# When eight small filler writes enter the transfer queue of a mixture-of-experts kernel

## The chip, the cores and the metric

The kernel runs on one core of a Trainium2 chip. The metric is the device time of one execution in microseconds (us); the number that counts is the median over several executions. Engines are named as in the profile: PE is TensorE (PEld its weight loads), DVE is VectorE, ACT is ScalarE, POOL is GpSimd, SP is SyncE, which in this kernel only issues transfers (DMAs). All data is float32.

## What is computed

One transformer layer: layer norm and cross attention (32 heads, 8 key and value groups) with a residual, then layer norm and a feed-forward block made of one shared expert and eight routed experts of which each token uses two. Cut to the part around the change:

```
x = x + xattn(layernorm(x), ctx, ctx, Wq, Wk, Wv, Wfc, bfc)      # 8 x 256 tokens, 512 wide
h = layernorm(x).reshape(2048, 512)
scores = softmax(h @ gate_weight.T)                              # 8 experts
w, i   = two best experts out of the two best of four groups
routed = sum over the two: w * (silu(h @ gate_w[i].T) * (h @ up_w[i].T)) @ down_w[i].T   # inner width 352
shared = (silu(h @ sh_gate_w.T) * (h @ sh_up_w.T)) @ sh_down_w.T                         # inner width 704
x = x + routed + shared
```

## The kernel before

**Two phases.** `attention` does the attention, the shared expert and the router for one batch after another. The router gives each token, for each of its two experts, a row in a table `rows` in device memory: expert `e` owns a stretch that begins at row `e * S_R`, and POOL scatters the normed token, its weights and its number there (`send`, L1173). When the last token has its place, `plan` (L1184 to L1267) works out on DVE where each expert's rows end (`t_end`) and which expert and first row each later tile of 128 rows has (`t_exp`, `t_row`).

`routed` then runs over tiles of 128 rows. The first eight tiles are the first 128 rows of expert 0, 1, ... 7, with addresses known when the program is built; tiles from number 8 on take expert and row out of the plan. A tile `i` goes through these helpers:

- `load(i)` (L407, L413) issues five transfers from `rows`: four of 64 KB into `xs`, and one of 8 KB into `mark`.
- `turn(i)` (L434 to L451) transposes `xs` on DVE into `rxT` and copies the weight and the token number.
- `up(i)` (L468, L483, L485) multiplies by gate and up weights on PE (`rg`), takes the silu on ACT (`rsg`) and the product on DVE (`ract`).
- `turn_act(i)` (L491 to L494) transposes `ract` on PE into `ra` and copies it on DVE to `raT`.
- `down(i)` (L499, L510, L513) multiplies by the down weights (`ro`), scales (`ry`) and lets POOL add the rows to the output.

`run` writes the order out by hand. At step `n` it issues the load of tile `n + 2`, turns tile `n + 1`, and runs up of tile `n`, down of tile `n - 1`, and the transpose of `ract(n)`. On DVE, in which order is fixed, `turn(n + 1)` therefore stands ahead of `ract(n)`; on PE `ra(n)` waits for `ract(n)`.

**Weights.** All routed weights stay in SBUF: `up_weights(e)` is one transfer of 1408 KB (L381) and `down_weights(e)` one of 768 KB (L384). Those of experts 0 to 2 are asked for at the end of the attention phase, with the loads of tiles 0 to 2; step `n` asks for those of expert `n + 3`. At step 5 `second` (L428, L429) fetches another 1408 and 768 KB for a tile that is shared by two experts.

**Empty rows.** An expert's last tile can reach past its rows. `blank` is a table of 64 rows of zeros in device memory with harmless token numbers, and for each expert one transfer copies it behind the expert's last row (L575, 132 KB, memory to memory). `value` reads the address on SP out of `t_end` (L372). `alone` says that the scatters and these eight writes need not wait for one another, since no two of them write the same row. It says nothing on loads, which read the same table `rows`.

**SP's queue.** All of these transfers are issued by SP in the order of the program. Before the change SP's order from the end of attention on is:

```
up(0) down(0) load(0) load(1) up(1) down(1) load(2) up(2) down(2)
8 x [ read t_end, blank -> rows ]
act of the last batch -> kept                       (L199, 768 KB)
step 0: up(3) down(3)
step 1: load(3) up(4) down(4)
step 2: load(4) up(5) down(5) ...
```

Here up(e) and down(e) stand for the weight transfers. Each of SP's transfers signals one of eight semaphores in turn.

Of the kernel before, what the change touches and what calls it, by code (L numbers as in the profile page):

```python
# [60 lines left out]
N_EXP, F = 8, 352  # L61
# [24 lines left out]
def xattn_ffn(  # L86
# [46 lines left out]
    )  # L133
    left.close()
    routed(
        ctx, tc, ps_m, wgu, wd, wsd, kept, ident,
        rows, t_exp, t_row, t_one, t_all, t_end, blank, out, tail, right,
# [211 lines left out]
def alone(tc, dma):  # L349
    tc.declare_no_dep(dma, group="rows", reason="no two of them write the same row")  # L350
    tc.add_to_no_dep_group("rows", dma)


def routed(
# [16 lines left out]
    def value(table, i, engine, top, p=0):  # L371
        return nc.values_load(  # L372
            table[p : p + 1, i : i + 1],
            engines=(engine,),
            min_val=0,
            max_val=top,
            skip_runtime_bounds_check_because=because,
        )

    def up_weights(e):  # L380
        nc.sync.dma_start(wgu_all[:, e], wgu[e])  # L381

    def down_weights(e):
        nc.sync.dma_start(wd_all[:, e], wd[e])  # L384
# [11 lines left out]
    def load(i):  # L396


        xs[i] = place(early, [P, P // BAND, P], "xs", f"xs{i}", 3)
        marks[i] = place(early, [P, W - D], "mark", f"mark{i}", 3)  # L400
        k = i - N_EXP
        step = R if k >= N_FULL else P
        for p in range(0, P, step):
            first = i * S_R if k < 0 else value(t_row, k, ENG.SP, N_EXP * S_R, p)
            some = slice(p // BAND, (p + step) // BAND)
            for r in range(NC):
                nc.sync.dma_start(  # L407
                    xs[i][r * BAND : (r + 1) * BAND, some],
                    rows[bass.ds(first, step), r * P : (r + 1) * P].rearrange(
                        "(m i) d -> i m d", i=BAND  # L410
                    ),
                )
            nc.sync.dma_start(marks[i][p : p + step], rows[bass.ds(first, step), D:])  # L413

    def two(a, m, b, n):

        t = others.tile([P, len(SCH) * (D + S)], F32, tag="two", name="two")
        return (
            t[:, : a * m].rearrange("p (a m) -> p a m", m=m),
            t[:, a * m : a * m + b * n].rearrange("p (b n) -> p b n", n=n),  # L420
        )
# [3 lines left out]
    def second(i):  # L425
        e = value(t_exp, i - N_EXP, ENG.SP, N_EXP - 1, R)
        seconds[i] = wgu_2, wd_2 = two(NC, 2 * F, len(FCH), D)
        nc.sync.dma_start(wgu_2, wgu[bass.ds(e, 1)].rearrange("o p c f -> p (o c) f"))  # L428
        nc.sync.dma_start(wd_2, wd[bass.ds(e, 1)].rearrange("o p c d -> p (o c) d"))  # L429

    def turn(i):

        xTs[i] = place(early, [P, NC, P // BAND, BAND], "xT", f"rxT{i}")
        nc.vector.transpose(  # L434
            xTs[i].rearrange("p c m i -> p m c i"),
            xs.pop(i).rearrange("p m (c j) -> p m c j", j=BAND),
        )
        row = marks.pop(i)

        w1s[i] = place(early, [P, 1], "w1", f"rw1_{i}", 5)  # L440
        if i < N_EXP:
            nc.vector.tensor_copy(w1s[i], row[:, i : i + 1])
        else:
            wt = place(early, [P, N_EXP], "wt", f"rw{i}")
            nc.vector.tensor_mul(wt, row[:, :N_EXP], t_one[:, i - N_EXP])
            nc.vector.tensor_reduce(w1s[i], wt, AX.X, ALU.add)
        ids[i] = []
        for part, _ in halves(i, None):
            to = place(early, [P, 1], f"id{part.start}", f"rid{i}_{part.start}", 6, I32)
            to = to[: part.stop - part.start]  # L450
            nc.vector.tensor_copy(to, row[part, W_ID - D : W_ID - D + 1].bitcast(I32))  # L451
            ids[i].append(to)
# [23 lines left out]
    def up(i):  # L476
        of_expert(i)
        gu = [ps_g.tile([P, F], F32, tag=f"g{k}", name=f"rg{i}_{k}") for k in range(2)]
        for k in range(2):
            product(gu[k], i, slice(k * F, (k + 1) * F))  # L480
        del xTs[i]
        sg = place(work, [P, F], "sg", f"rsg{i}")
        nc.scalar.activation(sg, gu[0], AF.Silu)  # L483
        acts[i] = place(work, [P, F], "act", f"ract{i}")
        nc.vector.tensor_mul(acts[i], gu[1], sg)  # L485
# [35 lines left out]
    def down(i):  # L521
        o = ps_y.tile([P, D], F32, tag="y", name=f"ro{i}")
        for fc, (_, fn) in enumerate(FCH):
            down_chunk(o, i, fc, fn)
        add_up(o, i)

    def last(i, before):


        of_expert(i)  # L530
        g = ps_g.tile([P, F], F32, tag="g0", name=f"rg{i}_0")
        product(g, i, slice(0, F))
        sg = place(work, [P, F], "sg", f"rsg{i}")
        nc.scalar.activation(sg, g, AF.Silu)
        down(before)
        a = place(work, [P, F], "act", f"ract{i}")
        aTs[i] = place(work, [P, len(FCH), P], "aT", f"raT{i}")
        o = ps_y.tile([P, D], F32, tag="y", name=f"ro{i}")

        def values_of(fc):  # L540
            f0, fn = FCH[fc]
            u = ps_g.tile([P, F], F32, tag=f"g{int(fc < 2)}", name=f"ru{i}_{fc}")[:, :fn]
            product(u, i, slice(F + f0, F + f0 + fn))
            nc.vector.tensor_mul(a[:, f0 : f0 + fn], u, sg[:, f0 : f0 + fn])

        def turned(fc):
            f0, fn = FCH[fc]
            ps = ps_m.tile([P, P], F32, tag="m", name=f"ra{i}_{fc}")
            nc.tensor.transpose(ps[:fn], a[:, f0 : f0 + fn], ident)
            nc.vector.tensor_copy(aTs[i][:fn, fc], ps[:fn])  # L550

        values_of(0)
        values_of(1)
        turned(0)
        values_of(2)
        turned(1)
        down_chunk(o, i, 0, FCH[0][1])
        turned(2)
        for fc in (1, 2):
            down_chunk(o, i, fc, FCH[fc][1])  # L560
        del xTs[i]
        add_up(o, i)
# [7 lines left out]
        up_weights(e)  # L570
        down_weights(e)

    for e in range(N_EXP):
        to = value(t_end, e, ENG.SP, N_EXP * S_R)
        alone(tc, nc.sync.dma_start(rows[bass.ds(to, R), :], blank).ins)  # L575
    while tail.cost < tail.total - 2 * 0.88:
        tail.step()
    turn(0)
# [30 lines left out]
    def run(tiles):  # L609

        halfs = [n for n, i in enumerate(tiles) if i >= N_EXP + N_FULL]
        when = [N_EXP - 3, *(n + 3 for n in halfs)]
        for n, i in enumerate(tiles):
            if 3 <= n + 2 < len(tiles):
                load(tiles[n + 2])
            if i + 3 < N_EXP:
                up_weights(i + 3)
                down_weights(i + 3)
            for k, at in zip(halfs, when):
                if at == n:  # L620
                    second(tiles[k])
            if n + 1 == len(tiles):
                last(i, tiles[n - 1])
                break
            if n == halfs[-1] + 2:
                down_sh, act_sh = two(len(SCH), D, len(SCH), S)
                nc.sync.dma_start(down_sh, wsd)
                nc.sync.dma_start(act_sh, kept)
            if n > 0:
                turn(tiles[n + 1])  # L630
            up(i)
            if n > 0:
                down(tiles[n - 1])
            else:
                turn(tiles[n + 1])
            turn_act(i)

        sums = []
        for q in range(QC):
            t0 = ((B - 1) * QC + q) * P  # L640
            to = out[t0 : t0 + P, :]
            sums.append((to, work.tile([P, D], F32, tag=f"sum{q}", bufs=1, name=f"sum{q}")))
            nc.sync.dma_start(sums[q][1], to)
        for q, (to, y) in enumerate(sums):
            ps = ps_m.tile([P, D], F32, tag="m", name=f"o{B - 1}_{q}")
            for i in range(len(SCH)):
                nc.tensor.matmul(  # L647
                    ps,
                    lhsT=act_sh[:, i, q * P : (q + 1) * P],
                    rhs=down_sh[:, i],  # L650
                    start=(i == 0),
                    stop=(i == len(SCH) - 1),
                )
            nc.vector.tensor_add(y, ps, y)
            nc.sync.dma_start(to, y)
        more()
# [4 lines left out]
    for k in range(RUN_HALF):  # L661
        tiles.insert(N_EXP + 4 + 7 * k, half[k])
    run(tiles)


# [825 lines left out]
```

## Time and profile before

| | us |
|---|---|
| median of 3 runs | 940.75 (939.1 to 941.12) |
| profiled execution, its own time | 938.76 |
| span of the profiled execution, first to last instruction | 937.0 |
| PE busy | 910.8 (97%) |
| DVE busy | 475.0 (51%) |
| ACT busy | 182.3 (19%) |
| POOL busy | 134.3 (14%) |
| mean granted TensorE clock | 0.993 |

The span is 1.8 us shorter than the profiled execution's own time, and that execution is 2.0 us below the median of the three runs. Times below are counted from the first instruction of the span. The routed phase begins on PE at 635.07 us, so it fills about the last third. The PE row of a profile counts time in which PE works; a time in which PE stands still while a transfer is under way shows as a dip in that row and as a step "DMA" in the chain of work that ended last.

### The profile page before, as it was taken

How to read it: one execution, taken by the hardware profiler on the slowest of the kernel's cores; microseconds unless marked ns; L12 is line 12 of the kernel's file. 1: busy time of each engine (PE TensorE's matmuls, PEld its weight loads, DVE VectorE, ACT ScalarE, POOL GpSimd, SP SyncE). 2: the span in 40 equal slices, each digit the busy share in tenths (PEclk: the TensorE clock that was granted, in tenths of full speed). 3: DMA queues.
4: the chain of work that ended last, by engine and by line, in shares of the span. 5: the costliest groups of instructions: out<-in, count | busy, mean ns of one | idle time of the engine just before them, and what ended most of it. 6: DMA issues, size and time to landing. Idle time of an engine off the chain costs nothing.

```text
span 937.0 us, 13140 instructions
## 1 busy us (share of the span) xinstructions
PE 910.8 (97%) x4865; PEld 531.1 (57%) x4865; DVE 475.0 (51%) x1063; ACT 182.3 (19%) x222; POOL 134.3 (14%) x171
## 2 busy tenths in 40 slices
PE   9999999999999999999999999999599999999997
PEld 8775565536445554654654544775355555555553
DVE  4554867566755856654675655382233333333331
ACT  1224123223223222222222241101000000000000
POOL 4000100201101101010120121030012212121211
PEclk9999999999999999999999999999799999999999
DMA  6366620201102021011111011069995364644623
GB/s 223 86 180 220 192 46 2 82 6 35 48 13 81 24 46 47 1 53 35 36 48 35 13 48 57 12 219 294 347 341 105 69 164 71 157 78 87 149 38 75
DMA packets 59266, 90.45 MB, mean 97 GB/s; under 512 B 13312, under 2 KB 39680, under 8 KB 57152
## 3 DMA queue, kind: packets, MB, share of 16 engines
q1 hardware_dynamic: 50512, 70.63, 24.7%
q0 software_dynamic: 7648, 17.83, 9.4%
q10 hardware_dynamic: 1040, 1.12, 0.4%
q8 instruction: 41, 0.67, 0.3%
q14 instruction: 25, 0.20, 0.1%
HBM read 57.88 MB, written 27.24 MB: 91 GB/s over the span
## 4 chain that ended last, share of the span: by engine, by line
PE 89%; DVE 4%; DMA 3%; SPq 1%; issue 1%; ACT 1%; POOL 0%; ACTq 0%; DVEq 0%; POOLq 0%
PE rg L468 16%; PE gu L181 14%; PE ro L499 9%; PE o L205 8%; PE s L988 7%; PE s L955 7%; PE fc L1046 6%; PE pq L921 6%; PE av L1007 6%; PE pkv L865 2%; DVE nm L964 1%; PE pkv L854 1%; PE ra L491 1%; PE o L647 1%; PE tn L972 1%; PE warm L1279 1%
## 5 line engine op out<-in xcount | busy, mean ns | idle before, releaser
L964 DVE TENSOR_REDUCE nm<-s 128x8 f32<-128x2048 f32 x64 | 146.6, 2290 | 86.2 <-PE s L955 82.0
L468 PE MATMUL rg<-wgu_all,rxT 128*128 (+2 forms) x552 | 171.3, 464 | 1.1 <-DVE rxT L434 0.9
L181 PE MATMUL gu<-hT,gu_w 128*128 128x256 f32 x704 | 166.6, 385 | 0.0
L996 ACT ACTIVATE ex<-s 128x2048 f32<-128x2048 f32 x64 | 120.1, 1877 | 225.7 <-PE s L988 216.0
L181 PEld LDWEIGHTS gu<-hT,gu_w 128*128 128x128 f32 x704 | 129.1, 190 | 40.9 <-issue 24.6
L468 PEld LDWEIGHTS rg<-wgu_all,rxT 128*128 128x128 f32 (+1 forms) x552 | 100.6, 187 | 56.4 <-issue 8.8
L499 PE MATMUL ro<-wd_all,raT 128*128 (+5 forms) x210 | 96.5, 594 | 0.0
L513 POOL DMA_INDIRECT y<-ry,rid x38 | 58.4, 1537 | 239.5 <-DVE ry L510 156.0
L205 PE MATMUL o<-down,act 128*128 128x512 f32 x168 | 79.6, 604 | 0.3 <-DVE q L346 0.3
L988 PE MATMUL s<-qT,kT 17*128 17x512 f32 x512 | 73.0, 640 | 2.0 <-DVE nm L964 1.9
L955 PE MATMUL s<-kT,qT 16*128 16x256 f32 x1024 | 73.4, 400 | 1.5 <-ACT ex L996 0.8
L483 ACT ACTIVATE rsg<-rg 128x352 f32<-128x352 f32 x34 | 15.8, 464 | 253.2 <-PE rg L468 246.0
L955 PEld LDWEIGHTS s<-kT,qT 16*128 16x128 f32 x1024 | 46.3, 184 | 30.9 <-ACT ex L996 14.1
L499 PEld LDWEIGHTS ro<-wd_all,raT 128*128 128x128 f32 (+3 forms) x210 | 38.4, 186 | 42.9 <-issue 35.5
L921 PE MATMUL pq<-xT,wq_sb 128*128 128x256 f32 x256 | 61.2, 386 | 0.5 <-DVE acc L214 0.3
L1007 PE MATMUL av<-ex,v 128*32 128x512 f32 x512 | 61.5, 598 | 0.0
L1046 PE MATMUL fc<-wfc_sb,o 128*128 128x512 f32 x128 | 60.9, 604 | 0.1
L1173 POOL DMA_INDIRECT rows<-lnf,idx x32 | 31.7, 991 | 201.0 <-DVE idx L1167 190.2
L485 DVE TENSOR_TENSOR ract<-rg,rsg 128x352 f32<-128x352 f32 x34 | 17.8, 523 | 84.0 <-PE rg L468 84.0
L510 DVE TENSOR_SCALAR ry<-ro,rw 128x512 f32<-128x512 f32 x35 | 26.3, 750 | 66.7 <-PE ro L499 66.7
L921 PEld LDWEIGHTS pq<-xT,wq_sb 128*128 128x128 f32 x256 | 46.6, 190 | 14.5 <-issue 6.0
L205 PEld LDWEIGHTS o<-down,act 128*128 128x128 f32 x168 | 29.4, 190 | 35.8 <-issue 34.5
(184 smaller groups left out, 710.0 us busy)
## 6 DMA issues: line engine op xcount, KB each, us to landing
wgu_all<-wgu SPq DMA_DIRECT2D x8, 1408.0 KB
xs<-rows SPq DMA_DIRECT2D x128, 64.0 KB
wd_all<-wd SPq DMA_DIRECT2D x8, 768.0 KB
two<-wgu SPq DMA_DIRECT2D x3, 1408.0 KB
cT<-ctxT SPq DMA_DIRECT2D x8, 512.0 KB
acc<-x SPq DMA_DIRECT2D x16, 256.0 KB
y<-acc SPq DMA_DIRECT2D x16, 256.0 KB
x<-x SPq DMA_DIRECT2D x14, 256.0 KB
```

Of the source, the lines that this page charges most:

```text
L181: nc.tensor.matmul(ps[:, i], lhsT=self.gu[k][:, c, i * P : (i + 1) * P], rhs=hT[:, c], start=(c == 0), stop=(c == NC - 1),)
L205: nc.tensor.matmul(ps, lhsT=act[:, k, q * P : (q + 1) * P], rhs=self.down[:, k], start=(i == 0), stop=(i == len(SCH) - 1),)
L468: nc.tensor.matmul(dst[part], lhsT=xTs[i][:, c, part.start // BAND : part.stop // BAND], rhs=w, start=(c == 0), stop=(c == NC - 1),)
L499: nc.tensor.matmul(o[part], lhsT=aTs[i][:fn, fc, part], rhs=w, start=(fc == 0), stop=(fc == len(FCH) - 1),)
L513: nc.gpsimd.indirect_dma_start(out=out, out_offset=bass.IndirectOffsetOnAxis(ap=to, axis=0), in_=y[part], in_offset=None, compute_op=ALU.add,)
L921: nc.tensor.matmul(ps[:, i], lhsT=wq_sb[:, c, part], rhs=xT[:, c], start=(c == 0), stop=(c == NC - 1),)
L955: nc.tensor.matmul(ps[:, r, j], lhsT=qT[band, G, j0 + j, qc * P : (qc + 1) * P], rhs=kT[band, G], start=True, stop=True,)
L964: nc.vector.tensor_reduce(nms[b, G, j0][:, qc], ps, AX.X, ALU.max, negate=True)
L988: nc.tensor.matmul(ps[:, r], lhsT=kT[band, G, kc * P : (kc + 1) * P], rhs=qT[band, G, j0 : j0 + 2], start=True, stop=True,)
L996: nc.scalar.activation(ex, ps, AF.Exp, scale=HD**-0.5)
L1007: nc.tensor.matmul(av[32 * r : 32 * r + 32], lhsT=vs[b % DEEP][:, kc, 4 * G + r], rhs=ex[:, r], start=(kc == 0), stop=(kc == QC - 1),)
L1046: nc.tensor.matmul(ps, lhsT=o[:, c, qc * P : (qc + 1) * P], rhs=wfc_sb[:, c], start=(c == 0), stop=(c == NC - 1),)
```

## The change

The eight writes of empty rows become a helper `empties(e)`, and they move. They were issued all together between the weights of expert 2 and `kept`. Now step `n` of `run` issues two of them behind its weights, for experts `2n` and `2n + 1`: two each at steps 0, 1, 2 and 3, and none later. The number, the size and the addresses of the writes are the same.

```diff
@@ routed
-    for e in range(N_EXP):
+    def empties(e):
+
         to = value(t_end, e, ENG.SP, N_EXP * S_R)
         alone(tc, nc.sync.dma_start(rows[bass.ds(to, R), :], blank).ins)
+
     while tail.cost < tail.total - 2 * 0.88:
         tail.step()
     turn(0)
@@ run
             if i + 3 < N_EXP:
                 up_weights(i + 3)
                 down_weights(i + 3)
+            for e in range(N_EXP)[2 * n : 2 * n + 2]:
+                empties(e)
             for k, at in zip(halfs, when):
                 if at == n:
                     second(tiles[k])
```

SP's order after it:

```
... load(2) up(2) down(2)
act of the last batch -> kept
step 0: up(3) down(3) blank 0, 1
step 1: load(3) up(4) down(4) blank 2, 3
step 2: load(4) up(5) down(5) blank 4, 5
step 3: load(5) up(6) down(6) blank 6, 7
step 4: load(6) up(7) down(7)
```

## The prediction

> **What bounds the kernel now.** First the page's slices, for where PE stands still:
>
> ```profile
> PE   9999999999999999999999999999599999999997
> PEclk9999999999999999999999999999799999999999
> DMA  6366620201102021011111011069995364644623
> ```
>
> A slice is 23.4 us. PE is full but for slice 29 (656 to 679 us), the start of the routed phase, where the granted clock falls too. DMA is at nine tenths in slices 28 to 30. Then the chain of waits around this dip:
>
> ```profile
> 651.97 3.81 DMA rows<-blank
> 655.80 0.33 SPq L407
> ...
> 657.52 8.64 DMA xs<-rows
> ...
> 667.19 0.44 DVE ract L485
> 667.63 0.04 issue
> 667.68 0.90 PE ra L491 x3
> 668.58 6.48 PE rg L468 x16
> 675.06 2.58 PE ro L499 x6
> 677.64 0.33 PE ra L491 x3
> ```
>
> PE's idle 11.1 us ends with `ra(2)`, which waits for `ract(2)`, which stands on DVE behind `turn(3)`, which waits for `xs` of tile 3. That load was issued at 655.80, when the last empty-row write had landed. So the writes are in the chain today. SP's part of the timeline:
>
> ```profile
> 640.59 0.33 SPq L384 DMA_DIRECT2D wd_all<-wd  x1
> 644.42 8.06 SPq L575 DMA_DIRECT2D rows<-blank  x8
> 652.57 0.53 SPq L199 DMA_DIRECT2D kept<-act  x1
> 653.15 0.45 SPq L381 DMA_DIRECT2D wgu_all<-wgu  x1
> 653.64 0.64 SPq L384 DMA_DIRECT2D wd_all<-wd  x1
> 655.80 2.15 SPq L407 DMA_DIRECT2D xs<-rows  x4
> ```
>
> The eight writes hold SP for 8.06 us, 1.0 us each. Two waits show. The first write begins only when the last piece of load(2) has landed (its semaphore is full at 644.29): a write waits for every earlier load of `rows`. And load(3) waits for the semaphore of the eighth write, although it reads the first 128 rows of expert 3: a load waits for earlier writes of `rows`. Lastly the windows of the transfers:
>
> ```profile
> 648.00:650.00 2.00, 2.00 (x9) 1.00 0.87 318
> 650.00:652.00 2.00, 2.00 (x8) 1.00 0.42 134
> 652.00:654.00 2.00, 2.00 (x8) 1.00 0.88 136
> 654.00:656.00 2.00, 2.00 (x6) 1.00 1.10 367
> ```
>
> The last two columns are DMA share and GB/s: a hole of some 4 us, because SP issues the small writes more slowly than they move, and then a full stream.
>
> From 656 to 706 us the routed phase lives on that stream. By the landings in the trace (last of 16 marks), mark of tiles 3, 4, 5, 6, 7 lands at 666.3, 673.7, 682.2, 690.2, 698.3: 8.0 us per tile, against 7.65 on PE (0.33 + 4.74 + 2.58 in the chain). The slack is used up by tile 8: `turn(8)` starts at 706.42, `ract(7)` ends at 707.87, PE is ready for `ra(7)` at 708.04. So each us by which the stream is later at tile 8 is a us of the end; a us earlier counts only if it is earlier there too.
>
> **The change, part by part.** *Removed:* 8.06 us of SP, and the hole. In order: down(2) stays at 640.59. `kept` follows, when down(1)'s semaphore is full at 643.08; up(3) and down(3) by 644.5; then two reads of `t_end` and two writes by 646.7. The stream doesn't stop now: down(2) lands at 650.8 as before, `kept` 2.4 later (before: 655.78 to 658.16), up(3) 3.8 later (658.16 to 661.95), down(3) 2.7 (to 664.68), two writes at 0.35 (successive writes at 651.45 and 651.77). Sum: 660.3.
>
> *Added: load(3) waits for writes 0 and 1, which lie behind up(3) and down(3) in the queue.* It goes out at 660.3, not at 655.8, but into an empty queue: its last `xs` is issued 1.7 us on and lands 1.85 later (706.92 to 708.75, an empty stretch), so 663.9 in place of 666.16. `ra(2)` comes at 665.4 instead of 667.7. So far a gain of 2.3 us.
>
> *Added: the same wait three more times, and its mirror.* Writes 2 and 3 wait for load(3) to land (T + 3.7, counting from the load's issue T). On SP up and down(4) are ahead of them, so nothing useful is held up; but their data queue behind those weights, and load(4) stands behind them on SP and waits until they have landed. All that comes after load(4), up(5) included, waits with it, and the queue runs dry. The period from load to load:
>
> - five issues of load: 2.3 us (664.75 to 667.02)
> - up from issue to landing in a nearly empty queue: 6.3 us (up(1): 634.25 to 640.57)
> - down: 2.5 us (up(1) at 640.57, down(1) at 643.08)
> - two writes: 0.7 us, and 0.1 until SP goes on
>
> Together 11.9, with POOL's scatters in the queues about 12.0, against 8.0 today. The writes' own issues (T + 3.8 to T + 5.8) lie beside the weights and cost nothing. Without cover they would cost 2 us a pair.
>
> So T is 660.3, 672.3, 684.3, 696.3 for loads 3 to 6. Their `xs` land 3.6 later: 663.9, 675.9, 687.9, 699.9. `ra(i)` follows 1.3 us after the landing of `xs(i + 1)` (666.38 to 667.68) if PE is ready: `ra(3)` at 677.2 (before 677.5), `ra(4)` 689.2 (685.1), `ra(5)` 701.2 (692.8). Load(7) waits for no write and follows up and down(7) in the stream (T + 11.2 + 1.5 = 709.0 against 698.3); the two transfers of `second` and load(8) follow at the 8.0 of today, 717.0 against 706.3. `ra(7)` comes at 718.3 against 708.04.
>
> **Sum: +10.3 us at tile 8, rounded to +10.** After it PE is the bound with full buffers as before (load(9) lands 5 us ahead of its use), so nothing is won back.
>
> *A rule on order.* In the trace writes issued from 644.42 on land behind down(2): the first write's marks begin at 648.56, down(2)'s at 648.26, 4 us after the write's issue. [...] If writes overtook the weights, they would land 3.2 us after issue (the seventh write, 650.94 to 654.16), at T + 8.0: the next load would be out before the weights are through, and the period would be today's. [...] I take the row, since the writes kept their place behind the weights there.
>
> *A rule on the clock.* The 11.1 us of idle PE were followed by half clock from 661.7 to 672.0, and `rg(3)` took 6.68 us instead of 4.90. [...] While the stream is the bound a tile at half clock (7.65 + 1.8 to 2.7) still fits into 12.0; only behind the last stop would 0 to 4 us come on top. [...]
>
> **The rivals.** *Faster: the transfers flow on.* One mechanism: no new load waits behind weights, because the writes land early or are not tied to them. Then `xs(3)` follows in the stream at 661.9, 4.3 earlier than today, and three more pairs of writes give back 3 x 0.7: -2.2 at tile 8, thus 938.6 us. For it: the hole of 4 us goes away with certainty. Against it: load(3) waits for the eighth write's semaphore today. It decides if a write lands within about 8 us of the load before it, or if load(4) is issued before down(4) has landed.
>
> *Only part of the stops.* The first pair gains as I say, but the period is nearer 9.5 to 10.5, since up takes 3.1 to 3.8 us once data flow and the latency is smaller behind the landing loads. Four periods then lose less: +3 to +6, about 945. Against it are up(0) and up(1), 6.1 and 6.3 us in nearly empty queues.
>
> *More.* Half clock behind the last stop, and slower writes: +13 to +17, about 955.5.
>
> **How the numbers follow.** The main case has 0.72 (its own range 947.5 to 953.5), part of the stops 0.12, faster 0.10, more 0.06. The profiled execution took 938.76 (span 937.0), so its twin would take 948.8; against the median of 940.75, 2.0 above that execution, the forecast is 940.75 + 10 = 950.7. The range 944 to 955 takes in the main case, most of the partial one and the edge of the last. What can be told from no change is about 0.2%, 1.9 us: faster by more has 0.09, within it 0.03 (the edges of the faster and the partial case), slower 0.88.
>
> **What would show it.** Right: `kept` issued near 643 us, up(3) right behind it; load(3)'s wait at L407 put down to the writes at about 660; loads 3 to 6 some 12 us apart; low DMA shares of 2 to 3 us around each; `ra(2)` about 2 us earlier; two or three PE idles of about 4 us, ended by `ract` behind `turn`, where there was one of 11. Wrong: loads 4 to 6 issued 8 us apart and one short PE idle (the faster rival), or PE idle at tiles beyond 8, which nothing in my sum makes.

## The result

The changed kernel takes 951.34 us (median of 4 runs, 949.07 to 952.2) against 940.93 (median of 4): 10.4 us slower, ratio 1.0107, 95% interval 1.008 to 1.0134. The forecast was 950.7. The profiled execution took 952.2, its span is 950.5. First the page's slices, now 23.8 us wide:

```profile
PE   9999999999999999999999999986779999999996
PEclk9999999999999999999999999999889999999998
DMA  6377610200101111102011001278786364644623
```

One slice of half-idle PE (slice 29 before) has become three of six or seven tenths (slices 28 to 30, 642 to 713 us), and the transfers, at nine tenths there before, are down to seven or eight. The chain of waits in that stretch says what PE waits for now:

```profile
646.67 12.29 DMA rows<-blank
658.98 0.35 SPq L407
...
660.80 1.88 DMA mark<-rows
...
663.92 7.77 DMA rows<-blank
...
671.77 0.34 SPq L407
...
676.67 6.66 DMA rows<-blank
...
688.26 8.77 DMA rows<-blank
...
697.10 0.33 SPq L407
```

Four times the chain goes through the landing of a write of empty rows; before it did so once. SP's timeline shows the order of issue (start, duration, line, names, count), with L576 for the writes (L575 before):

```profile
642.77 0.33 SPq L199 DMA_DIRECT2D kept<-act  x1
643.14 0.43 SPq L381 DMA_DIRECT2D wgu_all<-wgu  x1
643.62 0.43 SPq L384 DMA_DIRECT2D wd_all<-wd  x1
644.90 2.30 SPq L576 DMA_DIRECT2D rows<-blank  x2
658.98 1.77 SPq L407 DMA_DIRECT2D xs<-rows  x4
660.80 0.43 SPq L413 DMA_DIRECT2D mark<-rows  x1
661.27 0.43 SPq L381 DMA_DIRECT2D wgu_all<-wgu  x1
661.74 0.43 SPq L384 DMA_DIRECT2D wd_all<-wd  x1
662.83 1.58 SPq L576 DMA_DIRECT2D rows<-blank  x2
671.77 1.76 SPq L407 DMA_DIRECT2D xs<-rows  x4
```

SP issues nothing from 647.2 to 658.98, and again from 664.4 to 671.77. Its waits between 640 and 712 us, longest in total first, begin with

```profile
SPq L407 <- DMA rows<-blank: 33.5, 4, 11.8
```

33.5 us in four waits. The kernel before has one:

```profile
SPq L407 <- DMA rows<-blank: 1.4, 1, 1.4
```

Meanwhile the queue runs dry, as the windows show (last columns: granted clock, DMA share, GB/s):

```profile
654.00:656.00 2.00, 2.00 (x6) 1.00 1.08 360
656.00:658.00 2.00, 0.36 (x1) 1.00 0.61 157
658.00:660.00 2.00, 0.00 (x0) 1.00 0.03 7
660.00:662.00 2.00, 0.00 (x0) 0.65 0.56 130
```

PE's timeline has a stop in front of `ra` (L491) for each (in brackets the idle time before it and who ended it):

```profile
663.70 0.90 PE L491 MATMUL ra<-ident,ract 128*128 128x128 f32 x3 [7.34 <-DVE ract L485]
...
676.46 0.55 PE L491 MATMUL ra<-ident,ract 128*128 128x128 f32 x3 [3.07 <-DVE ract L485]
...
688.12 0.90 PE L491 MATMUL ra<-ident,ract 128*128 128x128 f32 x3 [2.11 <-DVE ract L485]
...
701.84 0.90 PE L491 MATMUL ra<-ident,ract 128*128 128x128 f32 x3 [4.29 <-DVE ract L485]
```

`ra(7)` comes at 719.40 (708.04 before), and the last matmul group of the kernel 11.1 us later than before (931.00 against 919.92): nothing between tile 8 and the end gives time back. The spans of these two executions differ by 13.5; the 2.4 left over are behind the last matmuls. Of these, 1.3 is the last scatter, which was slower to land in this execution (POOL issues it at 932.61, SP reads the output back at 938.88: 6.3 us, before 5.0). The medians, 10.4 apart, are the measure.

### The profile page after: what moved, and what is told of

Its sections match the earlier page's. It is cut to its first block, busy times and chain, and to the rows that moved or that the text cites. A ratio compares the mean times of both kernels' runs of the same rounds, so it can differ in the third digit from the quotient of the medians.

```text
span 950.5 us, 13138 instructions
## 1 busy us (share of the span) xinstructions
PE 915.6 (96%) x4865; PEld 533.0 (56%) x4865; DVE 475.6 (50%) x1063; ACT 182.3 (19%) x222; POOL 134.3 (14%) x171
## 4 chain that ended last, share of the span: by engine, by line
PE 83%; DMA 8%; DVE 4%; SPq 2%; ACT 1%; issue 1%; POOL 0%; ACTq 0%; POOLq 0%; DVEq 0%
PE gu L181 14%; PE rg L468 14%; PE ro L499 8%; PE o L205 8%; PE s L992 7%; PE s L959 7%; PE fc L1050 6%; PE pq L925 6%; PE av L1011 6%; DMA rows<-blank 4%; DMA xs<-rows 2%; PE pkv L869 1%; PE pkv L858 1%; DVE nm L968 1%; DMA y<-ry,rid 1%; SPq L407 1%
## 5 line engine op out<-in xcount | busy, mean ns | idle before, releaser
L468 PE MATMUL rg<-wgu_all,rxT 128*128 (+2 forms) x552 | 175.2, 472 | 1.9 <-DVE rxT L434 1.9
L468 PEld LDWEIGHTS rg<-wgu_all,rxT 128*128 128x128 f32 (+1 forms) x552 | 102.8, 192 | 58.9 <-issue 11.6
L434 DVE STREAM_TRANSPOSE rxT<-xs 128x512 f32<-128x512 f32 x35 | 24.5, 701 | 59.3 <-DMA xs<-rows 59.3
```

The source lines that it names most:

```text
L468: nc.tensor.matmul(dst[part], lhsT=xTs[i][:, c, part.start // BAND : part.stop // BAND], rhs=w, start=(c == 0), stop=(c == NC - 1),)
```

## Experiments

Medians of the kernel before lay between 939.8 and 942.9 in the three groups of runs below, so each ratio is taken to the runs of before on the same chip in the same group. Where rows of different groups are compared, it is by these ratios.

| run | writes | ratio to before (95%) |
|---|---|---|
| changed kernel | 4 pairs on SP, behind weights | 1.0107 (1.008 to 1.0134) |
| e1_one_stop | 8 at step 0 | 0.9977 (0.9966 to 0.9987) |
| e2_two_stops | 4 and 4 at steps 0, 1 | 1.0026 (1.0015 to 1.0038) |
| e9_one_each | 1 a step, steps 0 to 7 | 1.0189 (1.0169 to 1.0209) |
| e3_ahead | pairs ahead of the weights | 1.0093 (1.0064 to 1.0123) |
| e4_pool | pairs on POOL's queue | 1.002 (1.0004 to 1.0035) |
| e5_early | all 8 ahead of down(0) | 0.9957 (0.9942 to 0.9972) |
| e6_early_aside | as e5, and pairs to a table unread | 0.999 (0.9972 to 1.0009) |
| e7_early_two_queues | as e5, 4 of 8 on ACT | 0.9997 (0.9983 to 1.0012) |
| e8_early_six_two | as e5, 2 of 8 on ACT, placed later | 0.995 (0.9933 to 0.9966) |
| r_before | the kernel before again | 1.0011 (0.9996 to 1.0026) |

**How many loads wait.** The same eight writes, always behind the weights of a step, spread over one, two and eight steps (the change has four).

```diff
-            for e in range(N_EXP)[2 * n : 2 * n + 2]:
+            for e in range(N_EXP)[8 * n : 8 * n + 8]:   # e1_one_stop; 4 * n .. + 4: e2_two_stops; n .. + 1: e9_one_each
```

> All eight writes go behind up and down(3) at step 0; only load(3) then waits for writes that lie behind weights. Theory of the stops (a load waits for writes that wait behind weights, four times): one stop is left. The writes land near 661, load(3) goes out at 661 and its xs lands near 664.5 (666.2 before the change); up(4) lands near 669.6 (669.4), and from there all is as before the change: 941 us, 939.5 to 943. Rival (each write behind weights costs by itself, wherever it stands): still eight such writes, so about 951.

> Four writes each at steps 0 and 1, so loads 3 and 4 wait, 5 and 6 don't. Theory of the stops: load(4) goes out some 12.5 us behind load(3), then the stream flows at 8.0 a tile; xs of tile 5 lands near 685 (682.1 before the change), +3 at tile 8: 944 us, 942.5 to 946. With one stop at 941 and four at 951 the time should grow by about 3 to 4 us a stop. Rival (cost of each write): about 951.

> The changed kernel with one write a step over steps 0 to 7, not two over steps 0 to 3: as many writes, but loads 3 to 7 each wait for one behind weights, and write 5 holds the two transfers of step 5 until load(7) has landed. Theory of the stops (cost goes by the number of loads that wait behind weights, some 4 us each): a fifth stop and half a sixth, less 0.35 a step for the lighter pairs: 4 to 7 us slower than the changed kernel, ratio to the kernel before 1.014 to 1.019. Rival (cost by the number of writes behind weights): as the changed kernel or faster, 1.007 to 1.011.

Measured: 941.22, 945.41 and 957.38 us, with 942.88, 942.88 and 939.81 for before in their groups: -1.7, +2.5, +17.6 us; the change stands at +10.4. (The first two lie in the ranges expected; e9's ratio is at the upper end of its range.) The number of writes is the same in all, the number of loads that wait behind weights is one, two, four and five, with a sixth stop in e9 where write 5 holds the two transfers of step 5 (PE idles 5.22 us ahead of `ra(7)`). So time goes by waiting loads, about 4 us for each beyond the first, and not by writes. SP's waits of this kind in e1, e2 (640 to 712 us) and e9 (640 to 720 us), where the change has four:

```profile
SPq L407 <- DMA rows<-blank: 2.0, 1, 2.0
SPq L407 <- DMA rows<-blank: 14.5, 2, 9.6
SPq L407 <- DMA rows<-blank: 41.4, 5, 13.3
```

By its interval e1 is even a little faster than the kernel before. Its profile doesn't show why: `ra(7)` comes at 708.19, in two profiles of the kernel before at 708.04 and 710.44. It may be that the hole in front of `kept`, which is gone, cost more than one round trip; that is not shown.

**Which half of the wait.** A write waits for the load before it, and a load for the writes before it. In e3 the two writes stand ahead of the step's weights.

```diff
+            for e in range(N_EXP)[2 * n : 2 * n + 2]:
+                empties(e)
             if i + 3 < N_EXP:
                 up_weights(i + 3)
                 down_weights(i + 3)
-            for e in range(N_EXP)[2 * n : 2 * n + 2]:
-                empties(e)
```

> The two writes of each step stand ahead of the step's weights, so that they no longer queue behind them. They still wait for the load before them to land, and now the weights stand behind them on SP. Theory that both waits count (load on writes, writes on load, each with a stretch of the queue behind it): load(3) goes out early (about 652) and lands near 661, but up(4) is asked for only after that; the period is load's landing + two issues 2.1 + up 6.3 + down 2.5 + load in the stream 1.5 = 12.4 us, three times in place of four: +7.5, 948 us (946 to 951). Rival (only the place behind the weights costs): 939 to 941.

952.34 us. That is above the range expected (946 to 951), but before was at 942.88 in this group: +9.5 by medians, near the upper end of +5 to +10, and as slow as the change. The waits on SP swap their places (640 to 712 us):

```profile
SPq L576 <- DMA xs<-rows: 17.3, 3, 6.3
SPq L407 <- DMA rows<-blank: 9.0, 4, 4.9
```

Loads no longer wait long for writes; the writes wait for loads that lie behind weights, and the next weights stand behind the writes on SP. Loads 3 to 6 go out at 652.99, 664.75, 677.62 and 692.17, 13.1 us apart on average. Their place ahead of the weights helps the first and not the period.

**Another queue.** The writes from POOL's queue, with the same waits.

```diff
-        to = value(t_end, e, ENG.SP, N_EXP * S_R)
-        alone(tc, nc.sync.dma_start(rows[bass.ds(to, R), :], blank).ins)
+        to = value(t_end, e, ENG.Pool, N_EXP * S_R)
+        alone(tc, nc.gpsimd.dma_start(rows[bass.ds(to, R), :], blank).ins)
```

> The changed kernel with the writes issued from POOL's queue in place of SP's; the same waits of loads on writes and of writes on loads. Theory of the queue (the waits are long because the writes lie behind weights in SP's queue, and SP stands still meanwhile): in a queue of their own the writes land some 3 to 5 us after their issue, loads and weights flow on, the hole at 650 us is gone, xs of tile 3 lands near 661: 936 us, 934.5 to 940. Rival (the waits themselves, whatever the queue): about 951.

945.05 us, ratio 1.002: neither. Some 8 us of the loss are gone, but the 5 us of gain that I expected did not come. Its chain of waits:

```profile
656.43 6.39 DMA mark<-rows
...
664.44 4.01 DMA rows<-blank
668.50 0.33 SPq L407
...
670.37 1.74 DMA mark<-rows
...
673.80 5.33 DMA rows<-blank
679.18 0.33 SPq L407
```

Load(3) goes out at 654.60, 4.4 us earlier than in the change, since writes 0 and 1 no longer stand behind the weights of expert 3. From then on it is a loop: load lands, write goes out, write lands (4.0, 5.3 and 6.9 us after the second issue of each pair, with weights on their way at the same time), next load. Loads 3 to 6 are 13.9, 10.7 and 12.2 us apart, on average 12.3 where the change has 12.7. So the place in SP's queue is worth some 8 us, not the 15 that I expected: my theory of the queue held for the first stop only. For the later ones a load must wait for a write that must wait for a load, and while it waits, SP asks for no weights (it issues nothing from 658.33 to 668.50).

**Without the waits.** In e5 all eight writes go out ahead of all loads but behind up(0), where SP waits anyway for the plan; in e6 there are besides the change's four pairs, into a second table of the same size that nothing reads. Both are shown against the changed kernel; the lines that make the second table are left out.

```diff
     up_weights(0)
+    for e in range(N_EXP):
+        empties(e)
     down_weights(0)
...
-            for e in range(N_EXP)[2 * n : 2 * n + 2]:
-                empties(e)                                # e5_early
+            for e in range(N_EXP)[2 * n : 2 * n + 2]:     # e6_early_aside
+                to = value(t_end, e, ENG.SP, N_EXP * S_R)
+                alone(tc, nc.sync.dma_start(aside[bass.ds(to, R), :], blank).ins, "aside")
```

> No write stands between loads and weights: all eight follow up(0) on SP, ahead of down(0), where SP waits for the plan (617 to 628 us) in the kernel before. Loads 0 to 7 come behind them. Theory of the stops: load(0) waits till the last write has landed, near 631 (628.7 before the change), so some 2.5 us are lost there; after that no load waits behind weights, the hole at 650 us is gone, xs of tile 3 lands near 663 (666.2): about 3 us faster than the kernel before, ratio 0.995 to 0.998, one PE idle of 6 to 8 us. Rival (what makes the changed kernel slow is something other than the waits between loads and writes): no better than the kernel before.

> As e5_early, and besides the eight writes two at a time where the change puts them, but into another table that nothing reads (so they are added work, and nothing waits for them). This keeps the place, the bytes and SP's issues of the changed kernel and takes its waits away. Theory of the stops: 6 of the 8 writes lie in the stream ahead of load(6), at 0.35 us each: 1 to 2.5 us slower than e5_early. Rival (their place in the queue and their traffic cost by themselves): 10 us slower than e5_early, like the changed kernel.

e5: 937.09 us (before 940.45), 0.43% faster; of the versions so far only e1 was faster than the kernel before, by 0.23%. e6: 940.1, that is 3.0 us more than e5 and level with before. The added pairs have the change's place in the queue, its bytes and its issues on SP; without the waits they cost 3.0 us. That is more than the 1 to 2.5 expected. The changed kernel is some 14 us slower than e5 (ratios 1.0107 and 0.9957), so the other 11 us are what the waits make. Among SP's waits of e6 between 640 and 712 us there is none of a load on a write. PE's waits in e6 from 655 to 720 us show stops of little size behind the first:

```profile
PE ra L493 <- DVE ract L487: 7.8, 3, 5.7
```

**A better place.** In e5 the eighth write is issued at 630.54, so down(0) comes at 631.40 and load(0) at 633.01 (628.28 and 628.73 in the kernel before, in an execution whose attention phase was 1.8 us shorter). PE feels it: `ra(0)` comes 9.7 us behind the last matmul of attention, 6.6 in the kernel before. The later stop ahead of `ra(2)` is then only 3.81 us long, where I expected 6 to 8. Two attempts to shorten the delay put writes on ACT's queue; they are shown against e5.

```diff
     up_weights(0)
-    for e in range(N_EXP):
+    for e in range(0, N_EXP, 2):        # e7; range(N_EXP - 2) in e8
         empties(e)
...
         nc.vector.tensor_copy(t_end, behind)
+        for e in range(1, N_EXP, 2):    # e7: here; in e8 one step of plan later, for the last two alone
+            to = nc.values_load(t_end[0:1, e : e + 1], engines=(ENG.Activation,), ...)
+            alone(tc, nc.scalar.dma_start(rows[bass.ds(to, R), :], blank).ins)
```

> As e5_early, but four of the eight writes go out on ACT's queue as soon as t_end is there, the other four on SP behind up(0). They are through near 628, so load(0) is not held up: 2 us better than e5_early, about 5 us faster than the kernel before, ratio 0.993 to 0.996. If the stream after the hole is not what sets tile 8 once it starts earlier (PE at half clock, or PE's 7.65 us a tile, takes over), no better than e5_early.

> As e5_early, but two of the eight writes go out on ACT, placed behind the activation of 620.4 us so that they fit into the 3.07 us that ACT idles there; six stay on SP. In e7_early_two_queues four writes on ACT kept it for 4.5 us, and the plan on DVE and down(0) came 4 us late. If two fit, SP is through two writes earlier, load(0) goes out 1 to 2 us earlier than in e5_early: ratio to the kernel before 0.993 to 0.996. If ACT is late again, the plan is, and the ratio is 0.997 to 1.0.

e7: 939.52 us, 2.4 more than e5; the expected gain failed. ACT's timeline:

```profile
621.05 4.48 ACTq L1197 DMA_DIRECT2D rows<-blank  x4
625.58 0.66 ACT L193 ACTIVATE sg<-gu 128x256 f32<-128x256 f32 x2 [8.44 <-issue]
```

The four issues hold ACT for 4.5 us, the shared expert's activation behind them is late, DVE stands in front of the product that needs it (idle 4.44 us, to 625.99), the rest of the plan is behind that on DVE, and down(0), which waits for the plan, goes out at 633.00. In e8 two writes follow the activation and fit:

```profile
619.38 0.38 ACT L193 ACTIVATE sg<-gu 128x256 f32<-128x256 f32 x1 [3.65 <-PE gu L181]
620.09 2.60 ACTq L1224 DMA_DIRECT2D rows<-blank  x2
622.83 0.38 ACT L193 ACTIVATE sg<-gu 128x256 f32<-128x256 f32 x1 [3.07 <-PE gu L181]
```

934.86 us against 939.81, ratio 0.995: the fastest kernel of this study, 0.5% faster than the kernel before. It cannot be told from e5 by these intervals. Its PE timeline has one stop of 5.30 us in front of `ra(2)` and then none up to 740 us.

**The kernel before once more.**

> The kernel before once more, for a second profile on the chip of these runs: ratio 1, one PE idle of 10 to 12 us ahead of ra(2). If its median is above the profiled execution shown (938.76), the second profile tells where such executions lose time: in the attention phase, at the stop, or at the end.

Ratio 1.0011: the same kernel twice, so a tenth of a per cent between two rows of the table says nothing. Its profiled execution took 942.44 us and has one stop of 12.15 us ahead of `ra(2)` at 669.25, and `ra(7)` at 710.44, against 11.08, 667.68 and 708.04 in the profile shown at the top. So single executions differ by about 2 us in this very stretch; against the mean of both, `ra(7)` of the change is 10.2 us late, which agrees with the medians. Another 1.2 us of the second profile are lost behind the last matmuls.

## Why the prediction was right

The mechanism was the one forecast: four loads wait for writes that lie behind weights, and the queue runs dry each time. In the first full period the parts come as in the sum. Up(4) lands 9.1 us after load(3)'s issue, down(4) 2.3 later, the two writes 1.3 later, and load(4) goes out 0.1 after that; the forecast was 8.6, 2.5, 0.7 and 0.1. That the total is right within 1 us is in part luck: load(3) came 1.3 us earlier than forecast and the three periods were together 2.1 us longer, and these errors have opposite signs. Point by point, forecast and measured (start times in us):

| | forecast | measured |
|---|---|---|
| `kept`, and up(3) right behind | 643.1 | 642.77, 643.14 |
| load(3) | 660.3 | 658.98 |
| load(4), load(5), load(6) | 672.3, 684.3, 696.3 | 671.77, 683.39, 697.10 |
| `ra(2)` | 665.4 | 663.70 |
| `ra(3)`, `ra(4)`, `ra(5)` | 677.2, 689.2, 701.2 | 676.46, 688.12, 701.84 |
| `ra(7)` | 718.3 | 719.40 |

- *The hole goes, the first stop shrinks.* Right: `ra(2)` is 4.0 us earlier than in the profile of before, 1.7 more than forecast. Down(2) was through at 650.00, where I had taken over 650.8 from before, and of the four terms behind it three were a little smaller and one larger (down(3), 3.0 us for 2.7).
- *Four waits of loads on writes.* Right, four waits at L407.
- *The period of 12.0.* Measured 12.8, 11.6 and 13.7, on average 12.7. The last is the longest because up and down(6) landed 10.1 us after up(6)'s issue (685.68 to 695.75), where I had 8.8.
- *Slack at tile 8 and nothing won back.* Right: 11.4 at `ra(7)`, 11.1 at the last matmuls.
- *The order in the queue.* The writes kept their place, as I took it: writes 0 and 1, issued at 644.90 and 646.67, landed last at 658.63 and 658.96, right behind down(3) at 658.32. But by itself the place explains less than I thought: with the writes in another queue the forecast from the same reasoning was 936 us, and 945.05 came out (7 us off if taken to before in its group). The stop is a loop of load, write and load; the queue adds to it.
- *The clock.* The granted clock fell to 0.50 at all four stops, also at those of 2.11 and 3.07 us (see the last section). `rg` behind them took 6.1 to 6.6 us, 4.90 at full clock. In the trace it cost nothing, as `ra(3)` to `ra(6)` were each still ended by `ract` behind `turn`, the last one with 0.47 us to spare; no run here tries it by itself. No run shows the up to 4 us that might have come on top behind the last stop: `rg` was 1.2 us longer there, and `ra(6)` still waited for `ract`.
- *The faster rival* needed loads that do not wait. e6, with loads that don't, shows such a kernel: level with before. e5 and e8 show what was to be had from the 8 us of SP time: 3 to 5 us, by a place ahead of all loads.

## What to carry to other kernels

Before small writes are spread among reads of the same table, ask which waits the dependency tracking will put between them, in both directions: here eight writes in one lump held up one load, in four pairs four loads, and one by one five loads and a fetch of weights (the loads waited 2.0, 33.5 and 41.4 us on SP). When a load waited on SP, what stood behind it waited too, here 2176 KB of weights each time, for up to 11.8 us. If the data are ready early, look for a stretch where the issuing engine waits for something else: the 8.6 us of SP that the eight writes of e5 took went for the most part into a wait of 11 us that was there already. They delayed the first tiles by 3 us and still won 0.4% in all.

## What was not expected of the hardware

The granted clock fell also at short stops, and not at all of them. In the change PE idled for 2.11 us ahead of `ra(4)` (686.01 to 688.12) and the record has half clock (0.50) from 687.92 to 691.34; it idled 3.07 us ahead of `ra(3)` and half clock came at 677.68, 1.2 us after PE had gone on. In e7 PE idled 3.35 us ahead of `ra(2)` (663.86 to 667.21), and `rg` behind it took 4.90 us, as at full clock. So in these runs the length of a stop alone did not decide. What did is not shown; no run here varies a stop by itself.

Writes from POOL's own queue landed 4.0 to 6.9 us after issue, beside weights in SP's queue. In the change the second write of each pair, behind the weights on SP, took 12.3, 7.8, 6.7 and 8.8 us. In the kernel before, the seventh write from SP, of the same size, was issued at 650.94, while 134 to 136 GB/s were moved, and landed at 654.16, after 3.2 us. Why the writes on POOL's queue were not faster is open.
